# Four graph layers on one core: feed-forward offsets by accumulating DMAs, norm factor on ScalarE, minus the mean on VectorE, a new order table

## The chip, the cores and the metric

The kernel runs on one core of a Trainium2 chip. The metric is the device time of one execution in microseconds. Three executions of the kernel before took 4222.34, 4218.64 and 4213.73 us; the median is 4218.64. The engines are named as in the profile: PE (TensorE, matrix products), DVE (VectorE), ACT (ScalarE), POOL (GpSimd), SP (SyncE, which here only issues DMAs). "PEld" is the loading of weights into the array.

## What is computed

Sixteen graphs `b` of 1024 nodes with 256 features go through four layers that share one 1024 by 1024 adjacency matrix. Each layer has the form `x = x + layer(relu(layernorm(x)))`:

```python
# layers 0, 1 (one head) and 3 (four heads): graph attention
h = x @ W
e = leaky_relu(h @ a1 [:, None] + h @ a2 [None, :])
att = softmax(where(adj, e, -big));  out = relu or elu (att @ h)
# layer 2: eight heads of 32, then a feed-forward part with two norms
q, k, v = split(x @ w_qkv)
t = softmax(where(adj > 0, q @ k.T / sqrt(32), -1e9)) @ v
x = layernorm(x + t) * ln1_g + ln1_b
h = relu(x @ w1 + b1)
x = layernorm(x + h @ w2 + b2) * ln2_g + ln2_b
```

Everything is float32.

## The kernel before

**Stages.** One stage is one layer of one graph, 64 stages in all. The rows of a graph lie as eight tiles of 128 nodes (`NT = 8`), handled in two halves `n` of four tiles (`TH = 4`). The list `order` interleaves the stages: in the middle of the run (2, b), (1, b+1), (3, b), (0, b+2) follow each other, so one period of four stages handles one graph's worth of work, and the way into a stage (norm, transposes, products with the weights) runs under the stage before it.

**Who decides the order.** Nothing is issued directly. Every piece of work is laid down by `op(engine, cost, rank, function, after, ...)`: a planner's record with an engine, an assumed cost in us, what it needs and which buffers it takes. `play` then lists all records in one sequence, and the engines execute their share of it in that order. The sequence comes from `RANKS`, a table of three characters for each record. With another number of records the table cannot be used, so a change that adds or drops records brings a table of its own. The three PSUM double banks (`banks`), the two single ones (`bank`) and eleven large SBUF tiles (`large`) are shared by all stages and are handed out in the planner's order.

**Layer 2.** `dot_item` handles four heads, one tile of keys and one half of queries: eight score products (L1606, `sc`), two exponentials on ACT (L1620), two multiplications with the mask on DVE (L1628), and four products with the values (L1637, `acc`). The softmax sums need the same `pe` tiles again. To halve that work, POOL issues an accumulating DMA for each pair of items (`gather`, L1654: `pe` of the second item is added to `pe` of the first, 1 MB), and one set of products with a column of ones (L1667, `sums`) follows for the pair. There are 16 such gathers for each graph.

**The feed-forward part.** When half `n` of the attention is done, `dot_out` leaves `x + t` in `y`, and `feed_forward` and `finish` run for its four tiles:

- `stats_of`: DVE takes mean and variance (L1051, L1052), POOL makes `(var + eps) ** -0.5` in two instructions (L1055, L1056).
- `affine` on DVE: two instructions of 128 by 256, `(y - mean) * g1` (L1089) and `* rstd + be1` (L1090). `be1` there already holds `ln1_b + b2`, added once at the start; what this adds too much to the product with `w1` is taken off `b1` (`fold_bias`, L1930).
- PE turns the four tiles (L1099), ACT copies them (L1102), PE multiplies with `w1`, ACT applies bias and relu (L1765), PE multiplies with `w2`.
- `finish`: DVE adds the product to `y` with a running sum (L1788), POOL makes minus the mean of it (L1082), ACT the sum of squares about the mean (L1072), POOL the factor (L1075, L1076), DVE the second `affine` (L1089, L1090), and DVE adds the result to `x`, again with a running sum (L1808) for the next layer's norm.

`moments_of` with its POOL instruction L1082 also serves the norms of the layers 1, 2 and 3 on their way in (`way_in`). The running sums that it starts from are written by the last DVE instruction of the layer before (L1417 after layer 0, L1432 after layer 1, L1808 after layer 2).

**At the start**, weights and norm vectors are loaded by SP in four groups; two of the four norm vectors of the feed-forward part are the offsets `be1_sb` and `be2_sb`. **At the end**, the last stage (layer 3 of the last graph) has nothing beside it; DVE makes its weights `p` (L1452) and PE uses them in L1510 and L1486. After the loop six checks are reduced to one flag (L1973 to L1981), and an untaken slow path follows.

Of the kernel before, what the change touches and what calls it, by code (L numbers as in the profile page):

```python
# [26 lines left out]
F32 = mybir.dt.float32  # L27
BF16 = mybir.dt.bfloat16
U8 = mybir.dt.uint8
# [30 lines left out]
    "$;8#QT$Pe#,y#<<#)_#'C#'Z#%^$Qv#$}$%v#*Q#%K#7c#(D#'o#*n#(9#*d$RK#qb$N]$L{#(W#(J#(h#_S#(*#%E#(g#dC$HW#&F#(A#&q#)f"  # L60
    "$<k#)M#%V#'[#(##Xl#+0#X##e.#d}$RJ#+Z#(+#(/#W}#+/#$i#%S#+.#e(#e2#(c#(V#)c$Qy#',$Fn$K^$Cw$AK#()#(f#)v#%D#*J#pc$KY"
    "$=S$E[#)'#WB#)P$P^#),##S#)`#2d#qo#*z#$W#+S$Ey#'c$F%$87#'N#(w#*B#oe#*V$BH#W|$FI#mh#({#)#$(.#_R#*t$FB#WA$Ax##{#(^"
    "#(]$7Z#)S#c:#/i#V?#I*$95#)1#)2$(,$9S$Lu$7`##O$Av$:]#'r#US#-Z#*_#*'#6N#*C#):#+T#*N#+H#*L#*0#dv#*M#+E#)6#)U$(%$Qs"
    "#NY$BA$:E#Oy#&1#)Q#)^#.^$:0#){$#;$:$#)R#FV#'q#)x#)W#18#)p##&#Fi##1#7%#)F#)}#)r#HC#)7##,#4W##:#5?#*&#(L#.[$=U#)o"
    "#hf#+(#-p#)3$@t#*5$PX#aM#*<#)n#J`#pM$:r#)E#*Y##+$LK#*b#*/#'8$8`#D}#/A#*I#*E$O'#bg#ix#W##+?#+=#/;#(Y#)$#AW#7b#GL"
    "#Wy#*i#*a#K'#bf#hF#,;#+-#+G$8##+K#+$$@-#8H#-G#>S#)[#+#$?l#2I$IG#>G#+I#(1#+p$/]#$r#*}$%O#,-$?F#7.#+4#+6$>^#7#$')"
    "#mo#+Q$9c$JB#+b#+M#*4$2&#NJ$&p#*O#$q#mk#pU#/]#6c#+z#{J#z7#*f#%v#n##*v#@4#jM#%/#&P#8u$A5#?[#*u#,*$-p$/+#,>#%$#nN"
    "#68#9Q#+`#+k#+|#n|#,Y$-I#KF#,$$-H#69$7f#,E#,+#,m#,b#,I#,a#,k#+_#,f#,n$9>#,'#,p$-}#,{#,u#*Z#,t#,v#+N#,(#Iq#KI#,g"
    "#)@#Qz#*y#,:#4m#*.#/3#-/#.=#R*#&U#n)$8(#HT#.j#/^#.H#.6#0p#&o$F{#/m$Eu#/$#,4#0t#.h#.Q#Uy#)<#Rl#iY#/)#-a#-&#.p#.3"
    "#(Q#h0#Q.$Jn#-Q$Dc#-B#.>#0X#/d#0M#/g#/`#.k#PQ#.l#.M#GA#/8#/7#%.#p[#,8#-,#-Y#-)#-X#pE#nB#o,#/j#,H$L.$/Z#,P#+j#+<"  # L70
    "#03#-[#05#-7#+]#4>#02$My$=]#,U#@l$8L$4[#,`$)N#,j#3s#+J#-o#,K$8z#,l$Ly#+F#/.$9k#6F#/4#,Z#-s#-$$8;#-A#*q#+U$MK#-C"
    "$LT$@i#*8$=j$9i$;|#,<#-^$LS$E<$ML#,##+m#,}#ZO#+}#^T#-2#*p#,S#27#-F#*6#,O#-1#)l#-0#/+#(I#,c#*P#.8#,)#-x#.c#G`$?%"
    "#Om#.t#,6$>*#,F#P6#-:#0`#*7#&k#,9#7j#/f$;r#0Y#5N#/T#,V#.i#-q#08#.b#0E#*+#0$#*3#0*$<P#C7#2A#-R#'B#-e#.%#,_#-v#,B"
    "#,.#.K#-P#Q=#.{#.P#Q;#.O#.R#P(#.?#.}#Q3#-c#Py#8A#*)#?(#P%#-}#,A$22#--#.L#4v#/O#07#*l#3)#tO$2w#Rz#/V#3i$DF#/U#q)"
    "#0L#[s#/l#/G#^$#0-$G6#.*#0T#pf#/}#K(#/{#gZ#0?#-h#./#.&#q'#=r#q(#0w#*:#zc#(5#2R#3c#,i#,r#34#//#(k#+i$<)#*9#+3#-`"
    "#og#3@#-(#.9#'v#lW#:a#)z#(S#6>#*$#)9#Su#*%#+V#'R#*1#+r$$$#*[$,K#*w#)?#+a$?7#dx#+x$?v#+D#.r$LF#@G#.z#w/#Fx$>K$8t"
    "#(a#,[#*k#Sg#-y#df#,N#/?#-8$Kz#*D$L'#+;#?A#)|#,q#FK#aa#G2#+c$-z#/q#9S#l*#1/#Dd#uE#6:#,0#0;#]G#]F$:f#.-#,3#.4#.:"
    "#.2#.7#.;#.D#TV#mZ#0o#7^#,/#V;#9e#Q%#/K#mY#.S#.m$*,#/:#Un#Q2$Q<#.J#._#.u#.w#Q*#/=$2;$'N$Q;#/a$>m#mg#/H#Z*#/_#Q6"
    "#P_$2v$)w$Q}#Jb#zd#)w#+{#%X#+o#3J#*`#,^#,]#1<#m7#.E#-t#/Q#/-#/<#.0#/E$>r#/2$)1#s+$QV#_0#*##>*#$>#/Y#.|#97#tl#:X"
    "#.,#Vr#3*$Kg$/(#0x$Qm$J*#/w#32#)8#>)#c%#-|#2v$<}$80#/v#3?$7m#{+#0_#z^#oV#ur#+W#0n#4l#ou$PU#0m$';#,5#@6#On#Ro#1Q"  # L80
    "#Ps#DG#&>#.B#1j#1d#0]#1e#p|#.n#z;#1W#.1#/W$3l#ul#A:#1a#@`#0y#1P#/*#0{#0f#.W#0z#fc#-N$C)#G%$K@#0e#2##8j#1k#gz#6r"
    "#17#`c#39#2F#1T#21#/L#/B#/p#2J#0A#2D#1H$2I#2)#2B#2,#/s#2O#1^#0>#/n#1U#/o#2S#0u#1*$,9#1q$<;#2.#/S#2-#.y#1_#/1#bd"
    "#/@#0d#/D#b`#yi#2+#i*#bo#.o#-U#2*#0,##T#0%$=i#T9$9^#3m#i)#ew#/u#gn#E+#.F#8/#1(#/t#0(#0a#0'#2:$FZ#4'#kL#1E#+8#+f"
    "#s5$+*#s1#pN#22#/k#2Y#'*#y]#c}#zN#j*#2t#2f#-{#1:#-w#5t#pL#1I#1h#5}#a@#5k#1D#4G#4K#i%#3-#1S#ZH#19#fn#6G#1i#1F#aK"
    "#7_#fi#5W#]S#2&#gW#3v#m%#fl#-H#a?#7`#2n#15#ZG#7r$RD#;&$Bq#3Z$.7#3W#1o#f*#q-#F&#7s#3X#3B$%S#s.#F%#Q]#rf#yh#j##2r"
    "#$<#4&$,<#vv#QO#3>#3k#5J$)T#5X#QJ$.g#qU#4(#i$#5.#.e#5H$L(#3'#2l#3P#2j#30#2|#3Y#3S#3%$I'#2i#2g$GI#3O#3&#2o#2k#-f"
    "#4i#4V#^z#m.#4?#4L#24#1;#4U#5'#4t#6z#-M#g?#,|#4d#1R#rY#5)#51#+>#.+#gL#-n#(q#4r#Qg$N8#4}#54#4[#28#6j#.'$IO$@j#wr"
    "#5*#5;#4b#A[#4I#3H#1A#7F#0D#2G#66#77#6B#74#3_#5m$=>#5<#5/#6P#5z#5,#1M#pb$,>#w3#P}#7*#?<#0}#;Y#pF#.@#6o#3`#3K$,2"
    "#2W$F8$(3#4D$(}#0P#[r#m,#w.#10#>`$/P#2%#1z#GV#'g#/P$Ka#s$#0B#,C#'f#.N$L&#Li#a8$%@#3a#jG#6C#1)$2t#H|#3$$K`$L7#1G"
    "#LC$O$#3o#2y#2s$Cl#2x#5y#4Z#Ly$2s#5-#1s#@s#45#5P$Dy#4a$;7#5S#4P#2;#qZ$5u#M#$;0#5g$Cm$=5#6'#3}#W8#6@$P<#ei#5f#2>"  # L90
    "#3u#kB#4:#de#46#W`#44#1C#49#1,#e[#2[#_1#JG#6g#8<$*^#4S#y|#)-#I3#)s$*_#4,#3L#*K#I2#4e#7?#yy#6{#8?#1{#3<#/I#57#0&"
    "#5Q#6s#5C#5o#5D#gK#5_#5V#3h#5d#5I#LW#5T#5Y#?E#5+#0c#.#$<x#:|#4X#3y#5B#6*#5>#42#6##6.#41#9;$/Q#kp#6-#9}#43#5w#6H"
    "#5K#9I$1a#^x#6y#6L#:'#.Z#6]#pZ#6h#:Q#6k#:K#6Y#:&#6e#N&#5e#6d#3N#7/#3Q#2c#MI#2]#6;$Op#Yu#70#4h#4g#4w$?[#5c#3A#:q"
    "#sr$>'#S_#5=#G^$/2$1#$Iw#MK#(m#4c#4f#4`#5##4Q#4k#4B$4b$>P#4C#B`#52#56#f8#>}#f:#kA#/z#58#48#5Z#9.#Iw#98#60$?r#1Z"
    "#4)#8N#5v#63#6O$/<$9.#5L#}E#5x$9/#Bj#3]$9-#-j#=`#6$#:{$E'#8Z#3z#MA#6|#9j#5A#59#5G#61#p,$QB#5i#Bm$=^#5F#6b#9_#6T"
# [531 lines left out]
def fast_path(tc, bad, x, adj, l0_w, l0_a, l1_w, l1_a, w_qkv, ln1_g, ln1_b, ln2_g, ln2_b, w1, b1, w2, b2, l3_w, l3_a, out):  # L627
# [13 lines left out]
    with ctx:  # L641
# [1380 lines left out]
```

## Time and profile before

| what | us | where it is from |
|---|---|---|
| median of three executions | 4218.64 | times |
| the profiled execution | 4214.72 | times |
| its span | 4212.7 | page, part 1 |
| DVE busy | 3202.1 | page, part 1 |
| ACT busy | 2272.0 | page, part 1 |
| POOL busy | 1291.4 | page, part 1 |
| mean granted clock of TensorE | 0.996 | clocks and spans by core |

The profiled execution took 2.0 us longer than its span and 3.9 us less than the median. The span runs from the first to the last instruction; sums over the trace are compared with it. Busy time counts an engine as busy from the start to the modelled end of each instruction. Since matmuls follow each other in the array before the earlier ones have ended, a short wait of PE can hide behind the end of the matmul before it; the time from start to start is the safer measure there.

### The profile page before, as it was taken

Reading aid. Unit: us, or ns where it says so; the run is one execution under the profiler, and the core shown is the slowest. Engines: PE = TensorE matmul, PEld = TensorE weight load, DVE = VectorE, ACT = ScalarE, POOL = GpSimd, SP = SyncE. Lnnn points to the kernel's source line nnn. Section 1 sums busy time; section 2 is a strip of 40 time slices with the busy share of each in tenths; the row PEclk is TensorE's granted clock in tenths of the full one; section 3 lists DMA queues with packets and bytes.
Section 4 is the critical chain, followed back from the end, with each engine's and each line's share of the span. In section 5 each row is a group of like instructions: output and inputs, shape, how many; then the busy total and the mean of one; then the engine's idle time right before and its main releaser. Section 6 shows DMA issues by size and latency. Waiting matters only on the chain.

```text
span 4212.7 us, 67513 instructions
## 1 busy us (share of the span) xinstructions
PE 4106.9 (97%) x25993; PEld 2166.0 (51%) x25993; DVE 3202.1 (76%) x5708; ACT 2272.0 (54%) x4107; POOL 1291.4 (31%) x2473
## 2 busy tenths in 40 slices
PE   8999999999999999999999999999999999999997
PEld 7736265553645536455354654546545455564332
DVE  7477877778777787767877778787786777858797
ACT  5563646636465464654646546464563745665452
POOL 3325141422414133142232423223232242424231
PEclk9999999999999999999999999999999999999999
DMA  3061714418053180540805317062260723535261
GB/s 114 16 141 41 158 43 98 93 46 165 21 116 77 45 165 26 115 91 26 165 26 122 85 45 147 26 138 68 62 130 26 154 52 84 107 82 109 70 122 42
DMA packets 96457, 364.35 MB, mean 86 GB/s; under 512 B 10376, under 2 KB 45568, under 8 KB 63360
## 3 DMA queue, kind: packets, MB, share of 16 engines
q0 software_dynamic: 36864, 268.45, 31.7%
q1 hardware_dynamic: 58848, 90.98, 6.3%
q8 instruction: 207, 3.39, 0.3%
q14 instruction: 122, 1.00, 0.1%
q10 hardware_dynamic: 416, 0.52, 0.0%
HBM read 74.32 MB, written 17.17 MB: 22 GB/s over the span
## 4 chain that ended last, share of the span: by engine, by line
PE 76%; DMA 7%; DVE 6%; issue 5%; ACT 3%; POOL 2%; POOLq 0%; ACTq 0%; SPq 0%; DVEq 0%
PE pm L1106 20%; PE av L1388 19%; PE acc L1486 11%; PE sc L1606 7%; DMA pe<-pe 7%; PE acc L1637 6%; PE sums L1510 5%; PE tp L1099 3%; DVE pe L1628 3%; PE sums L1667 3%; ACT pe L1620 1%; POOL rstd L1076 1%; PE tpv L1549 1%; PE tpo L1686 1%; POOL pe L1654 1%
## 5 line engine op out<-in xcount | busy, mean ns | idle before, releaser
L1628 DVE TENSOR_TENSOR pe<-pe,mask 128x1024 f32<-128x1024 f32 x1024 | 1200.6, 1219 | 217.4 <-ACT pe L1620 213.9
L1620 ACT ACTIVATE pe<-sc 128x1024 f32<-128x1024 f32 x1024 | 997.6, 1023 | 331.0 <-PE sc L1606 202.1
L1388 PE MATMUL av<-v,p 128*128 128x257 f32 x4096 | 950.9, 382 | 6.9 <-ACT o L1411 4.3
L1388 PEld LDWEIGHTS av<-v,p 128*128 128x128 f32 x4096 | 760.6, 190 | 194.1 <-issue 56.1
L1452 DVE SCALAR_TENSOR_TENSOR p<-r,e,mask 128x1024 f32<-128x1024 f32 x512 | 622.5, 1273 | 113.4 <-DMA r<-kept 92.0
L1606 PE MATMUL sc<-qT,kT 32*128 32x512 f32 x4096 | 634.0, 641 | 2.7 <-ACT pe L1620 1.2
L1637 PE MATMUL acc<-pe,v 128*32 128x512 f32 x4096 | 543.9, 603 | 3.2 <-DVE pe L1628 1.9
L1654 POOL DMA_DIRECT2D pe<-pe x256 | 225.2, 882 | 933.6 <-PE acc L1637 616.0
L1486 PE MATMUL acc<-p,v 128*32 128x512 f32 x4096 | 467.6, 593 | 0.0
L1082 POOL TENSOR_SCALAR stats<-stats 128x1 f32<-128x1 f32 x512 | 166.4, 333 | 886.0 <-DVE x L1417 564.2
L1606 PEld LDWEIGHTS sc<-qT,kT 32*128 32x128 f32 x4096 | 194.9, 183 | 381.6 <-issue 185.2
L1106 PE MATMUL pm<-l_wx,hT 128*128 128x259 f32 (+1 forms) x1536 | 366.9, 388 | 3.8 <-ACT hT L1102 1.4
L1076 POOL TENSOR_TENSOR rstd<-rstd,minus_half 128x1 f32<-128x1 f32 x512 | 353.4, 690 | 42.7
L1371 DVE SCALAR_TENSOR_TENSOR p<-r,e,mask 128x512 f32<-128x512 f32 x512 | 351.1, 742 | 12.9 <-DMA r<-kept 11.1
L1106 PEld LDWEIGHTS pm<-l_wx,hT 128*128 128x128 f32 x1536 | 287.0, 190 | 74.2 <-ACT hT L1102 19.1
L1667 PE MATMUL sums<-pe,pick 128*32 128x512 f32 x2048 | 272.5, 600 | 39.0 <-DMA pe<-pe 38.3
L1486 PEld LDWEIGHTS acc<-p,v 128*32 128x32 f32 x4096 | 133.0, 110 | 295.2 <-issue 280.4
L1637 PEld LDWEIGHTS acc<-pe,v 128*32 128x32 f32 x4096 | 98.2, 108 | 349.4 <-issue 212.9
L1075 POOL TENSOR_SCALAR rstd<-stats 128x1 f32<-128x1 f32 x512 | 175.0, 342 | 275.6 <-ACT xn L1072 143.3
L1510 PE MATMUL sums<-p,e 128*32 128x512 f32 x2048 | 248.5, 596 | 6.0 <-DVE p L1452 6.0
L1055 POOL TENSOR_SCALAR rstd<-stats 128x1 f32<-128x1 f32 x256 | 94.2, 368 | 478.3 <-DVE stats L1052 472.5
L1106 PE MATMUL pm<-hT,qkv_sb 128*128 128x512 f32 x512 | 231.1, 597 | 2.3 <-ACT hT L1102 2.3
(119 smaller groups left out, 4271.4 us busy)
## 6 DMA issues: line engine op xcount, KB each, us to landing
pe<-pe POOLq DMA_DIRECT2D x256, 1024.0 KB, 8.4
r<-kept SPq DMA_DIRECT2D x64, 512.0 KB
x<-in_x_dram SPq DMA_DIRECT2D x32, 512.0 KB
out_dram<-x SPq DMA_DIRECT2D x64, 256.0 KB
r<-kept SPq DMA_DIRECT2D x62, 256.0 KB
edges<-in_adj_dram SPq DMA_DIRECT2D x8, 512.0 KB
kept<-rows_sb SPq DMA_DIRECT2D x128, 2.0 KB
qkv_sb<-in_L_gnn_w_qkv_dram SPq DMA_DIRECT2D x1, 768.0 KB
```

The source lines that it names most:

```text
L1076: nc.gpsimd.tensor_tensor(rh.t, rh.t, minus_half, ALU.pow)
L1106: nc.tensor.matmul(dst, lhsT=lhsT[:, k, :], rhs=rhs[:, k, :], start=(k == 0), stop=(k == KC - 1))
L1371: nc.vector.scalar_tensor_tensor(ph.t[:, j % each, :], rh.t, s.e[:, j, H + h : H + h + 1], mask[:, j, cols], ALU.max, ALU.mult)
L1388: nc.tensor.matmul(avh.t[:, : s.hs + 1], lhsT=phs[part].t[:, j % each, i * P : (i + 1) * P], rhs=s.v[:, j, h, :], start=(j == 0), stop=(j ...
L1452: nc.vector.scalar_tensor_tensor(ph.t[:, hh, :], s.rh[hp].t[:, hh, :], s.e[:, j, col : col + 1], mask[:, j, :], ALU.max, ALU.mult)
L1486: nc.tensor.matmul(acc[n].t[(2 * hh + part) * W : (2 * hh + part + 1) * W, :], lhsT=s.v[:, jj, h, part * W : (part + 1) * W], rhs=p, start ...
L1510: both(lambda jj, n, hh, h, p: nc.tensor.matmul(sums.t[(2 * n + hh) * W : (2 * n + hh + 1) * W, 0, :], lhsT=s.e[:, jj, 2 * H + h : 2 * H + ...
L1606: nc.tensor.matmul(scs[pair].t[:, hh, :], lhsT=s.kh.t[r0 : r0 + D2, g, j * P : (j + 1) * P], rhs=s.qh.t[r0 : r0 + D2, g, cols], start=True ...
L1620: lambda pair=pair: nc.scalar.activation(part(pair), scs[pair].t, AF.Exp, scale=SCALE2),
L1628: lambda pair=pair: nc.vector.tensor_tensor(part(pair), part(pair), masks(), ALU.mult), [ex], tiles=True,
L1637: nc.tensor.matmul(head(acc, i), lhsT=s.v[:, j, g * QUAD + i, :D2], rhs=ph.t[:, i, :], start=(j == 0), stop=(j == NT - 1))
L1667: nc.tensor.matmul(head(sums, i), lhsT=pick[:, g, :], rhs=th.t[:, i, :], start=first, stop=last)
```

## The change

The reference is unchanged. Six things differ.

- The two offsets of the feed-forward part, `ln1_b + b2` and `ln2_b`, are written once to DRAM as `offsets`, repeated for the four tiles of a half, by eight DMAs of SP. For each half of each graph POOL issues two accumulating DMAs of 512 KB (`offset`): one adds `ln1_b + b2` to the half of `y` after its transposes have been copied, the other adds `ln2_b` to the half of `x` after the tiles have gone through the norm of layer 2. The addition of the product with `w2` waits for the first, the last addition to `x` for the second. `b1` now gets `w1.T @ ln1_b` added.
- First norm of the feed-forward part: DVE keeps `(y - mean) * g1`, which no longer waits for POOL's factor; ACT multiplies with the factor. The second DVE instruction is gone.
- Second norm: DVE keeps `(y - mean) * g2`; the factor is applied in the addition to `x`, which was there before. The second DVE instruction is gone.
- Minus the mean (`mean_of`) is a DVE instruction of one column directly behind the running sum, no longer one of POOL. This holds for the layers 0, 1 and 2.
- Some assumed costs in the planner's records have other values.
- `RANKS` is new: 12154 entries, where there were 12409.

```diff
-        g1_sb, be1_sb = spread(ln1_g, "g1_sb"), spread(ln1_b, "be1_sb")
-        g2_sb, be2_sb = spread(ln2_g, "g2_sb"), spread(ln2_b, "be2_sb")
...
+        g1_sb, g2_sb = spread(ln1_g, "g1_sb"), spread(ln2_g, "g2_sb")
...
+        offsets = dram.tile([2, P, TH, C], F32, name="offsets", bufs=1)
...
-            r_op = op(POOL, 1.15 if shift else 0.85, rank + 0.6, root, [m_op], ends=[mh])
+            r_op = op(POOL, 1.1, rank + 0.6, root, [m_op], ends=[mh])
...
+        def mean_of(mh):
+            nc.vector.tensor_scalar(mh.t[:, 0:1], mh.t[:, 2:3], -1.0 / C, None, ALU.mult)
...
-            m_op = op(
-                POOL, 0.25, rank,
-                lambda: nc.gpsimd.tensor_scalar(mh.t[:, 0:1], mh.t[:, 2:3], -1.0 / C, None, ALU.mult), after,
-            )
-            q_op = op(ACT, 0.45, rank + 0.4, square, [m_op], takes=[rh, *takes], ends=ends)
-            r_op = op(POOL, 1.15 if shift else 0.85, rank + 1.0, root, [q_op], ends=[mh])
+            q_op = op(ACT, 0.49, rank + 0.4, square, after, takes=[rh, *takes], ends=ends)
+            r_op = op(POOL, 1.4 if shift else 1.15, rank + 1.0, root, [q_op], ends=[mh])
...
-        def affine(y, m, r, g, b, op0=ALU.subtract):
-            nc.vector.scalar_tensor_tensor(y, y, m, g, op0, ALU.mult)
-            nc.vector.scalar_tensor_tensor(y, y, r, b, ALU.mult, ALU.add)
...
+        def offset(s, n, which, after, rank):
+            ts = slice(n * TH, (n + 1) * TH)
+            def start():
+                nc.gpsimd.dma_start(out=(s.y, xs[s.b])[which][:, ts, :], in_=offsets[which], accum_op=ALU.add)
+            issued = op(POOL, 0.9, rank, start, after + [offsets_kept], delay=0.6)
+            return op(QUEUE, 2.7, rank, lambda: None, [issued])
...
+                centred = op(
+                    DVE, 0.4, at + 0.6,
+                    lambda yt=yt, mh=mh: nc.vector.scalar_tensor_tensor(
+                        yt(), yt(), mh.t[:, 0:1], g1_sb, ALU.subtract, ALU.mult
+                    ), [m_op] + folded[:1], ends=[mh], takes=[xh, uh] if i == 0 else [], tiles=True,
+                )
                 normed = op(
-                    DVE, 0.96, at + 2.0, lambda yt=yt, mh=mh, rh=rh: affine(yt(), mh.t[:, 0:1], rh.t, g1_sb, be1_sb),
-                    [r_op] + folded, ends=[mh, rh], takes=[xh, uh] if i == 0 else [], tiles=True,
+                    ACT, 0.4, at + 2.0, lambda yt=yt, rh=rh: nc.scalar.activation(yt(), yt(), AF.Copy, scale=rh.t),
+                    [r_op, centred], ends=[rh],
                 )
...
+            shifted = [offset(s, n, 0, [turned], rank + 1.0), offset(s, n, 1, [s.norms[n * TH + i] for i in range(TH)], rank)]
...
-                c = op(DVE, 0.8, rank + 3.7 + 4.0 * u, add, [a], takes=mhs)
+                        mean_of(mh)
+                c = op(DVE, 0.8, rank + 3.7 + 4.0 * u, add, [a, shifted[0]], takes=mhs)
...
+                    def add_scaled(xt=xt, yt=yt, nh=nh, rh=rh):
+                        nc.vector.scalar_tensor_tensor(
+                            xt(), yt(), rh.t, xt(), ALU.mult, ALU.add, accum_out=nh.t[:, 2:3]
+                        )
+                        mean_of(nh)
...
+                        DVE, 0.5, at + 3.0, add_scaled, [centred, r_op, shifted[1]], takes=[nh], ends=[s.yh, rh], tiles=True
...
+        def keep_offsets():
+            for i, row in enumerate((offset_in[:, 0, :], offset_2)):
+                for t in range(TH):
+                    nc.sync.dma_start(out=offsets[i, :, t, :], in_=row)
+        offsets_kept = op(SP, 2.0, 13.0, keep_offsets, [summed] + weights_in[0], ends=[ab_held])
```

In the order that the new table gives, each engine's instructions stand as follows beside the order before. POOL issues the two DMAs for `x` of a graph shortly before its layer 2 begins, the DMA for the first half of `y` between the last but one (or two) gathers of layer 2, and the one for the second half after the last gather. The eight writes of `offsets` stand on SP between the write of the first kept row (L1315 before) and the load of it (L1329 before). PE changes its tile shape 1352 times, before 1332 times; 511 blocks of scores are left, before 504.

## The prediction

> **What bounds the kernel now.** I read the busy times first.
>
> ```profile
> span 4212.7 us, 67513 instructions
> PE 4106.9 (97%) x25993; PEld 2166.0 (51%) x25993; DVE 3202.1 (76%) x5708; ACT 2272.0 (54%) x4107; POOL 1291.4 (31%) x2473
> ```
>
> PE is busy for all but 105.8 us, so no work that the change takes from DVE or POOL can come off the span directly. It pays only where PE waited for it. Hence the list of PE's waits:
>
> ```profile
> PE sums L1667 <- DMA pe<-pe: 38.3, 40, 2.7
> PE tp L1099 <- ACT xn L1160: 9.5, 5, 7.7
> PE count L1980 <- DVE broken L1978: 7.2, 1, 7.2
> PE sums L1510 <- DVE p L1452: 6.0, 2, 5.6
> ```
>
> The largest is for the gathers. This list misses waits that hide behind a matmul's modelled end, so I also costed every PE instruction at its undisturbed pace. The timeline shows the pace: 48 products of 257 columns start within 10.44 us, 217 ns each (0.84 ns a column); four products of a quarter of the array run abreast; a change of tile shape adds 0.09 us, leaving a block of scores 0.21 us, the second pair of scores of an item 0.10 us. All instructions of the trace cost 3996 us that way. PE starts at 7.7 us and the last instructions take 6.5 us; the rest, about 202 us, is waiting. Put to the instruction that started late: 62 us before the 256 groups of gathered sums (L1667), about 40 before scores, 28 before the projections L1106, 21 before L1388, some 25 in the last 130 us. 202 us, 4.8% of the span, is all that any order could win.
>
> Where the waits lie shows in one period (graph 4), cut at its gathers:
>
> ```profile
> core 0: us, PE busy (x) PEld busy (x) DVE busy (x) ACT busy (x) POOL busy (x), PEclk, DMA share, GB/s
> 1216.00:1266.00 50.00, 49.22 (x369) 16.03 (x361) 42.12 (x42) 36.86 (x46) 9.24 (x12) 1.00 0.96 198
> 1266.00:1311.00 45.00, 42.90 (x285) 16.13 (x288) 41.09 (x72) 26.31 (x41) 21.13 (x37) 1.00 0.83 167
> 1311.00:1380.00 69.00, 68.60 (x317) 50.27 (x313) 41.11 (x113) 36.53 (x85) 26.14 (x67) 1.00 0.09 32
> ```
>
> Of the 3.3 us lost, 2.9 fall into layer 2, where the DMA engines are 83 to 96% busy and DVE 84 to 91%. These two, not PE's neighbours in general, are what PE meets.
>
> **The change part by part.** The rows that price it:
>
> ```profile
> L1090 DVE SCALAR_TENSOR_TENSOR y<-y,rstd,be_sb 128x256 f32<-128x256 f32 x256 | 124.2, 485 | 43.1 <-POOL rstd L1076 19.6 <-POOL rstd L1056 0.9 <-POOL rstd L1075 0.9
> L1236 DVE TENSOR_SCALAR both<-e,rstd 128x4 f32<-128x4 f32 (+1 forms) x256 | 50.4, 216 | 66.7 <-ACT e L1231 58.5 <-POOL stats L1082 4.9 <-POOL stats L1078 1.2
> L1160 ACT ACTIVATE xn<-x,stats 128x256 f32<-128x256 f32 x256 | 125.8, 507 | 184.7 <-DVE stats L1052 179.6 <-DMA be_sb<-in_L_gnn_ln_b_dram 0.8
> L1082 POOL TENSOR_SCALAR stats<-stats 128x1 f32<-128x1 f32 x512 | 166.4, 333 | 886.0 <-DVE x L1417 564.2 <-DVE x L1432 135.0 <-DVE y L1788 94.9
> L1654 POOL DMA_DIRECT2D pe<-pe x256 | 225.2, 882 | 933.6 <-PE acc L1637 616.0 <-DVE pe L1628 211.2 <-issue 49.0
> ```
>
> *DVE.* 256 instructions L1090 go. One starts 0.40 us before the next, or 0.57 with the bubble of its dependence on L1089: 102 to 146 us, I take 115. 512 `mean_of` come. No such row exists; the nearest, L1236, takes 0.216 us but lets the next start after 0.08 to 0.13, and a dependent pair adds a bubble: 41 to 118 us, I take 67. Net 48 us less DVE work, between 105 less and 16 more. It lies beside PE everywhere; only the 91% stretch of layer 2 could pass some on. Its 3 us in each graph's stretch against 2.1 us of PE loss give 0 to -10 us; I take -2.
>
> *ACT* gains 128 copies like L1160, 65 us. ACT is 58 to 74% busy in the two stretches above, which covers them. Queued behind a copy that waits for POOL's factor are exponentials, and behind those the masks on DVE; with that cover gone four copies delay each of 32 halves by 2 us at most, on a quarter of them 16 us. I take 0 (0 to +16).
>
> *POOL* loses 512 x 333 ns = 170 us and gains 64 issues at 0.88 us, 56 us. It is 31% busy. The step from running sum to square (L1072) loses an engine change, 0.5 us or so. The chain ends before PE's queue of other work does; 0.
>
> *The offset DMAs in the gathers' queue.* This queue is the dear resource:
>
> ```profile
> q0 software_dynamic: 36864, 268.45, 31.7%
> pe<-pe POOLq DMA_DIRECT2D x256, 1024.0 KB, 8.4
> ```
>
> 31.7% of 4212.7 us over 256 gathers is 5.2 us each, and where gathers queue they are issued 5.2 us apart. 16 of them fill 83 of layer 2's 97 us. By size an offset costs 2.6 us; a price above a gather's 5.2 has no row for it. The two for `x` and the second for `y` fall where no gather is due. The first for `y` stands before the last one or two gathers of each graph. POOL executes in order: while that issue waits for the copied transposes (L1102), the next gather and the factors L1055 and L1075 stand behind it, and behind the gather the sums L1667. In PE work at undisturbed pace, the last three gathers now have 14.8, 14.6 and 12.3 us between the products that free them and their sums (before 11.1, 9.9, 8.9), while the shortest landing is 6.9 us. 2.6 us fit. With the cover gone, 16 x 2.6 = 42 us. I take +2 (0 to +42). The addition L1788 waits for the same DMA, but transposed copy, `w1`, relu and `w2` (0.9 + 3.4 + 0.7 + 3.5 us) lie between.
> The Trainium skill ("DMA: Bandwidth & Descriptors", Anatomy of one DMA) fits such a DMA by 2.0 us plus bytes over 436 GB/s. As an estimate from that page an offset would last 3.2 us and a gather 4.4; the shortest gather here takes 6.9, so the fit is low for accumulation, and by it the +2 stays.
> A rule against the change stands in "SBUF — State Buffer" (the warning on DVE and SWDGE): descriptors of POOL's DMAs cannot be written while certain DVE instructions hold the shared port. L1654's issues here take 850 to 1209 ns with DVE at 84 to 91%. By the rule 64 more issues could each stall an instruction's length; by the row 0.36 us at most.
>
> *SP's eight writes* stand before the load of the row for stage (0, 1). At the 0.4 us that earlier issues of this size take, the load is 3.2 us later, and so the weights that DVE makes of it. PE still has the first stage then: +1 (0 to +4).
>
> *The order table* is the largest part. Three things can be counted in the two orders of instructions.
> Tile shape: 7 more blocks of scores at 0.21 us, 13 other changes at 0.09: +2.7 us.
> Gathers: I binned the 62 us of waits by the PE work between the freeing products and the sums. Under 7 us: 9 groups, 0.9 us of wait each; 7 to 8: 30 at 0.60; 8 to 9: 58 at 0.35; 9 to 10: 62 at 0.16; above: 97 at 0.05. The new order has 3, 14, 57, 59 and 123: 2.7 + 8.4 + 20.0 + 9.4 + 6.2 = 47 us, so -15. Counting also the 5.2 us that each gather holds the queue leaves -5; counting that 27.6 us of the waits stood before the last two gathers, now the roomiest, gives -25.
> PSUM: a block that reuses a bank less than 1.5 us after its last writer lost 0.24 us (82 cases; now 56), scores within 1 us 0.71 (8; now 1): -11; some of these are gathered sums, so -9 (-12 to 0).
> The end: these lines show the last stage.
>
> ```profile
> 4151.12 1.89 PE L1510 MATMUL sums<-p,e 128*32 128x512 f32 x2 [5.58 <-DVE p L1452]
> ...
> 4149.70 31.17 DVE L1452 SCALAR_TENSOR_TENSOR p<-r,e,mask 128x1024 f32<-128x1024 f32 x26
> ```
>
> From the transposed row (4141.1) to the checks PE has 47.5 us of work but DVE needs 32 weights at 1.2 us plus 8.5 us until the row is back, so PE waits 5.6 + 2.3 us and then 0.3 us a dozen times. In the new order 59.5 us of PE work stand behind that transpose, more than DVE's chain takes: -8 (-12 to +3).
>
> **Sum:** 2.7 - 15 - 9 - 8 + 1 - 2 + 0 + 2 = -28 us. On the profiled span 4212.7 that makes 4185 us, 4187 with the 2.0 us around it; that execution lies 3.9 us under the median, which becomes 4190 us. All favourable ends together (-25 - 12 - 12 - 10 + 3) give 4163.
>
> **The rivals.** *Slower, 0.16:* the first `y` offset is the bound. For it speaks that layer 2's queue is already 83 to 96% full and that POOL waits in order; against it that the last gathers now have 12 us or more. It decides once an offset delays the next gather by over 5 us, 12.3 less the 6.9 of a landing. At 5.2 us more than covered on each of 16 graphs it costs 83 us against 30 won: 4270; at half of that, 4230.
> *No change, 0.14:* the distances count PE work alone, and DVE, also nearly full in layer 2, takes over as what ends the waits (L1628 before gathers and `acc`). Then only the end and the tile shapes remain, -8 + 3 + 1: 4215.
> *Much faster, 0.13:* assumed costs nearer to the rows (POOL's factor 1.1, rows 368 + 764 ns; before 0.85) let the table dissolve also the waits that I could not count, before projections and L1388 (49 us) and half of those before scores: 4190 - 40 - 10 = 4140.
> That the change does not do what it says is excluded by the listed order.
>
> **How the numbers follow.** The forecast, 4190, has 0.57; its own range is 4163 to 4209. A measurement tells about 0.2% (8.4 us) from no change. Faster: 0.57 + 0.13 = 0.70, same 0.14, slower 0.16. The range reaches half into the outer cases: 4148 to 4232.
>
> **What would show it.** Right: waits at L1667 under 30 us on the list, the wait for L1452 gone, PE busy unchanged within 10 us, the last gathers of a graph landing before their sums. Wrong: gathers behind the `y` offset landing after 12 us with sums waiting; POOL waiting at that issue for L1102's copies; PE waiting for DVE masks in layer 2; an offset taking as long as a gather.

## The result, and the profile after

| kernel | median us | executions | ratio to before, 95% interval |
|---|---|---|---|
| before | 4215.58 (4211.55 to 4222.34) | 12 | |
| after | 4213.69 (4205.08 to 4220.53) | 12 | 0.9993 [0.9984, 1.0002] |

No change that can be measured; 4190 was forecast. The profiled execution of after took 4213.85 us, 4212.1 of them its span, at a granted clock of 0.994 (the mean share of its full clock that TensorE was given).

The page of after, its first lines and its DMA queue:

```profile
span 4212.1 us, 67534 instructions
...
PE 4093.9 (97%) x25993; PEld 2160.5 (51%) x25993; DVE 3170.0 (75%) x5964; ACT 2322.9 (55%) x4235; POOL 1169.6 (28%) x2025
...
q0 software_dynamic: 46080, 302.01, 36.5%
```

The engines moved as the change says: DVE 32 us less, ACT 51 more, POOL 122 less, 33.6 MB more in the gathers' queue. The span did not move. So work went, and waiting came. The list of PE's waits of after (total us, times, longest):

```profile
PE sums L1658 <- DMA pe<-pe: 27.8, 35, 2.5
PE pm L1097 <- ACT hT L1093: 15.0, 18, 1.4
PE tp L1090 <- ACT xn L1151: 13.3, 9, 7.6
PE av L1379 <- ACT o L1402: 10.7, 9, 5.6
PE tps L1677 <- ACT sums_sb L1668: 7.4, 5, 5.7
PE count L2002 <- DVE broken L2000: 7.2, 1, 7.2
```

(L1658, L1097, L1090, L1379 and L1677 are L1667, L1106, L1099, L1388 and L1686 of before.) The wait for gathers fell from 38.3 to 27.8 and the 6.0 us at the end are gone, both as forecast. New are 10.7 us of `av` for `o` (4.3 before) with a single wait of 5.6, 15.0 of `pm` (5.5 before) and 5.7 of `tps` in one wait. The two lines of before:

```profile
PE pm L1106 <- ACT hT L1102: 5.5, 6, 1.2
PE av L1388 <- ACT o L1411: 4.3, 8, 1.6
```

The list misses waits behind modelled ends, so here is the accounting of the prediction again. It is worked out from the starts in the traces (start to start against the undisturbed pace) and is an estimate, not a view; the column of scores holds about 52 us that are pace, not waiting:

| waiting of PE, us | all | gathered sums | `av` | projections `pm` | `tps` and `tpo` | `acc` | scores | last sums |
|---|---|---|---|---|---|---|---|---|
| before | 254.5 | 62.1 | 20.9 | 27.6 | 9.6 | 8.2 | 93.0 | 9.2 |
| after | 249.0 | 40.7 | 38.3 | 39.1 | 15.6 | 4.1 | 87.6 | 1.6 |
| e1, below | 226.4 | 34.7 | 29.4 | 38.0 | 8.2 | 7.7 | 85.4 | 2.2 |
| e5, below | 235.8 | 51.3 | 24.7 | 39.0 | 10.2 | 3.1 | 83.9 | 1.5 |
| e11, below | 257.8 | 51.8 | 30.9 | 41.5 | 9.2 | 12.0 | 88.2 | 1.5 |

21.4 us before the sums, 7.6 at the end and 5.4 before scores were won; 17.4 before `av`, 11.5 before the projections, 6.0 before `tps` and `tpo` were given back, and 3.0 before the transposed masks, which have no column. All waiting fell by 5.5 us and the span only by 0.6, since the added changes of tile shape take 2.7 us and the part behind PE's last instruction 2.4 more (6.7 us before, 9.1 after).

What makes `av` late is found by following its longest wait, 5.56 us up to 1058.17 us. The chain of waits of after there (start us, length us, what):

```profile
1036.04 14.88 DMA y<-offsets
...
1053.11 0.61 ACT pm L1071 x2
...
1054.78 0.74 DVE p L1362
1055.52 0.41 DVE x L1819 x2
...
1057.75 0.37 ACT o L1402
...
1058.17 5.93 PE av L1379 x13
```

The offset for the first half of `y` takes 14.88 us, and from its landing the chain runs through the addition, the squares, the second norm and `o` into the wait of `av`. POOL's timeline of after (start us, length us, what, and in brackets the idle time before) says why a 512 KB transfer takes so long:

```profile
1030.58 0.86 POOL L1645 DMA_DIRECT2D pe<-pe  x1 [2.70 <-DVE y L1751]
1035.50 0.85 POOL L1645 DMA_DIRECT2D pe<-pe  x1 [4.07 <-PE sc L1597]
1036.04 1.21 POOL L1733 DMA_DIRECT2D y<-offsets  x1
```

It is issued half a microsecond after a 1 MB gather, and three gathers have not landed yet. By the trace they land at 1038.14, 1043.08 and 1048.43 us, some 5 us apart, and the offset 2.5 us behind the last, at 1050.92. And DVE:

```profile
1039.43 5.38 DVE L1362 SCALAR_TENSOR_TENSOR p<-r,e,mask 128x512 f32<-128x512 f32 x8
1051.02 0.42 DVE L1797 SCALAR_TENSOR_TENSOR y<-y,pm 128x256 f32<-128x256 f32 x1 [6.20 <-DMA y<-offsets]
```

Eight masks, then 6.20 us of nothing, then the addition at the moment of landing. The list of DVE's waits says how often that happens:

```profile
DVE y L1797 <- DMA y<-offsets: 17.7, 5, 6.2
```

In 5 of the 16 graphs the first addition starts 0.1 us after the landing of its offset, and DVE had stood for it: 5.5, 1.8, 6.2, 1.6 and 2.6 us in the graphs 1, 2, 3, 12 and 13 (counted from 0). In the other 11 it starts 0.2 to 4.9 us after the landing, held by its product or by DVE's other work. The offset of the first half lands 11.6 us after its issue in the median (5.5 to 17.1); the one for the second half, with no gather ahead, after 5.5 (5.3 to 6.0).
The Trainium skill ("DMA: Bandwidth & Descriptors", Anatomy of one DMA) fits such a DMA by 2.0 us plus bytes over 436 GB/s, as an estimate 3.2 us for 512 KB; the 5.5 us measured alone differ from it, and the fit has no term for what is ahead in the queue, which is the larger part of 11.6.

This wait of PE cost more than its length. The same 16 products `av` behind the wait, in after and then in e1 (below), where that offset is left out:

```profile
1058.17 6.60 PE L1379 MATMUL av<-v,p 128*128 128x257 f32 x16 [5.56 <-ACT o L1402]
```

```profile
1047.74 3.75 PE L1379 MATMUL av<-v,p 128*128 128x257 f32 x16
```

They take 6.60 us in place of 3.75. The granted clock (third column from the right) was 0.50 there in after (1.00 in e1):

```profile
1050.00:1057.20 7.20, 2.61 (x20) 0.74 (x18) 5.33 (x21) 3.42 (x11) 2.93 (x6) 1.00 0.65 134
1057.20:1064.00 6.80, 5.83 (x14) 4.63 (x15) 5.85 (x19) 4.59 (x14) 5.54 (x11) 0.50 0.01 2
```

The clock records of the trace hold 54.2 us at a clock of 0.5 in after, in stretches of 3.4 us or several of that which begin during a wait of PE or shortly behind one; 39.3 us in before, 31.7 in e1. The accounting above counts slow products as waiting.

### The profile page after: what moved, and what is told of

Read it like the earlier page. It is cut to its first block, busy times and chain, and to the rows that moved or that the text cites. A ratio compares the mean times of both kernels' runs of the same rounds, so it can differ in the third digit from the quotient of the medians.

```text
span 4212.1 us, 67534 instructions
## 1 busy us (share of the span) xinstructions
PE 4093.9 (97%) x25993; PEld 2160.5 (51%) x25993; DVE 3170.0 (75%) x5964; ACT 2322.9 (55%) x4235; POOL 1169.6 (28%) x2025
## 4 chain that ended last, share of the span: by engine, by line
PE 74%; DMA 7%; DVE 6%; issue 6%; ACT 4%; POOL 2%; SPq 0%; POOLq 0%; ACTq 0%; DVEq 0%
PE pm L1097 19%; PE av L1379 18%; PE acc L1477 10%; PE sc L1597 8%; PE acc L1628 6%; DMA pe<-pe 5%; PE sums L1501 5%; PE sums L1658 3%; PE tp L1090 3%; DVE pe L1619 2%; DMA y<-offsets 2%; ACT pe L1611 1%; DVE y L1797 1%; ACT pm L1071 1%; PE tpv L1540 1%
## 5 line engine op out<-in xcount | busy, mean ns | idle before, releaser
L1379 PE MATMUL av<-v,p 128*128 128x257 f32 x4096 | 956.7, 384 | 21.7 <-ACT o L1402 10.7
L1379 PEld LDWEIGHTS av<-v,p 128*128 128x128 f32 x4096 | 764.9, 191 | 210.9 <-issue 60.8
L1597 PE MATMUL sc<-qT,kT 32*128 32x512 f32 x4096 | 620.9, 642 | 2.7 <-ACT pe L1611 1.5
L1074 POOL TENSOR_SCALAR rstd<-stats 128x1 f32<-128x1 f32 x512 | 159.0, 311 | 1153.4 <-ACT xn L1071 739.8
L1097 PE MATMUL pm<-l_wx,hT 128*128 128x259 f32 (+1 forms) x1536 | 369.5, 389 | 8.1 <-ACT hT L1093 5.2
L1075 POOL TENSOR_TENSOR rstd<-rstd,minus_half 128x1 f32<-128x1 f32 x512 | 331.6, 648 | 42.7
L1097 PEld LDWEIGHTS pm<-l_wx,hT 128*128 128x128 f32 x1536 | 287.4, 191 | 79.1 <-ACT hT L1093 20.7
L1658 PE MATMUL sums<-pe,pick 128*32 128x512 f32 x2048 | 269.5, 603 | 28.6 <-DMA pe<-pe 27.8
L1051 POOL TENSOR_SCALAR rstd<-stats 128x1 f32<-128x1 f32 x256 | 131.9, 515 | 454.5 <-DVE stats L1048 450.8
L1097 PE MATMUL pm<-hT,qkv_sb 128*128 128x512 f32 x512 | 228.6, 593 | 2.6 <-ACT hT L1093 2.3
L1052 POOL TENSOR_TENSOR rstd<-rstd,minus_half 128x1 f32<-128x1 f32 x256 | 207.8, 812 | 21.3
```

What stands on the lines that cost most here:

```text
L1075: nc.gpsimd.tensor_tensor(rh.t, rh.t, minus_half, ALU.pow)
L1097: nc.tensor.matmul(dst, lhsT=lhsT[:, k, :], rhs=rhs[:, k, :], start=(k == 0), stop=(k == KC - 1))
L1379: nc.tensor.matmul(avh.t[:, : s.hs + 1], lhsT=phs[part].t[:, j % each, i * P : (i + 1) * P], rhs=s.v[:, j, h, :], start=(j == 0), stop=(j ...
L1597: nc.tensor.matmul(scs[pair].t[:, hh, :], lhsT=s.kh.t[r0 : r0 + D2, g, j * P : (j + 1) * P], rhs=s.qh.t[r0 : r0 + D2, g, cols], start=True ...
L1658: nc.tensor.matmul(head(sums, i), lhsT=pick[:, g, :], rhs=th.t[:, i, :], start=first, stop=last)
```

## The experiments

All are edits of after unless said otherwise; ratios are to the kernel before, run on the same chip (after: 0.9993). An edit's change against after is the difference of the ratios times 4216 us.

**e1 and e2: leave DMAs out.**

```diff
             def start():
+                if which == 0 and n == 0:
+                    return
                 nc.gpsimd.dma_start(...)
```

e2 has the `return` without the condition.

> The accumulating DMA of the first half of y is left out in every graph (ln1_b + b2 is not added there); the order of everything else is the changed kernel's. Theory A (that DMA lands behind one or two gathers, 10 to 17 us after its issue, DVE stands at L1797 until it lands, and the work behind DVE's wait makes PE late): about 25 us less than the changed kernel, 4190 us, DVE's idle time before the addition down from 85 to about 50 us, PE's waits before L1379 down from 38 to about 20 us. Theory B (the ACT copies and the table itself cause the new waits): within 6 us of the changed kernel, 4208 to 4218. Theory C (the DMA's 2.6 us in the queue delay the gathers behind it): the gain shows at the gathered sums, not at L1379.

> All 64 accumulating DMAs are left out (the offsets are not added); order as in the changed kernel. Theory A: the same as without the first y DMA alone, within 4 us, about 4188, since the other 48 land alone in 5.4 us where nothing waits long. If the traffic itself counts (theory C): at least 8 us less than without the first y DMA alone.

e1: 4188.41 us, 0.9937 [0.9920, 0.9953]. e2: 4190.12, 0.9943 [0.9927, 0.9960]. So the 16 transfers for the first half of `y` cost 0.9993 - 0.9937, about 24 us, and the other 48 nothing that can be measured. Theory A's time was met; DVE's idle time (69.8 us, below) and `av` in the accounting (29.4 us) fell less than it said. DVE's rows for the addition, after and then e1 (busy us, mean ns, idle before and its releasers):

```profile
L1797 DVE SCALAR_TENSOR_TENSOR y<-y,pm 128x256 f32<-128x256 f32 x128 | 52.9, 413 | 85.4 <-PE pm L1097 67.4 <-DMA y<-offsets 17.7 <-ACT pm L1071 0.2
```

```profile
L1799 DVE SCALAR_TENSOR_TENSOR y<-y,pm 128x256 f32<-128x256 f32 x128 | 52.9, 414 | 69.8 <-PE pm L1097 69.5
```

The 17.7 us of standing for the DMA are gone and 2.1 us come back as waiting for the product (67.4 to 69.5), so DVE stands 15.6 us less. By the accounting `av` wins 8.9 us, `tps` and `tpo` 7.4, the gathered sums 6.0.

**e3: the offsets added by DVE**, with one 128x1024 instruction at the place where the DMA was issued. This is the whole computation.

```diff
+                if which == 0 and n == 0:
+                    nc.vector.tensor_tensor(s.y[:, ts, :], s.y[:, ts, :], off_sb.unsqueeze(1).to_broadcast([P, TH, C]), ALU.add)
+                    return
```

> In the place of the DMA of the first half of y, DVE adds ln1_b + b2 with one instruction of 128 x 1024 (some 1.2 us, 16 times); all is computed. Theory A: it keeps most of the gain, 8 to 20 us less than the changed kernel, 4195 to 4206, less than both kernels; what is lost against leaving the DMA out is at most DVE's 16 x 1.2 = 19 us. Theory B: 4213 or up to 10 us more.

4194.18 us, 0.9950 [0.9933, 0.9967]: 0.5% less than before and 0.4% less than after. The 16 instructions take 1.22 us each, 19.5 us in all, and cost 6 us against e1.

**e4: minus the mean back on POOL**, in after's order (`mean_of` on `nc.gpsimd`).

> Minus the mean goes back to POOL (512 instructions of some 333 ns), at the same places of the order; all is computed. Theory A: this part of the change is worth little, 0 to 12 us more than the changed kernel. If the 512 small DVE instructions (79 us of DVE) are what gave the gain back: 10 to 25 us less than the changed kernel.

4249.02 us, 1.0084 [1.0067, 1.0100], 38 us slower than after: missed. The releasers of e4's second norm:

```profile
L1819 DVE SCALAR_TENSOR_TENSOR x<-y,rstd,x 128x256 f32<-128x256 f32 x128 | 61.5, 483 | 40.2 <-POOL rstd L1075 38.2
```

DVE now stands 38.2 us for POOL's factor there (11.7 in after), and PE's wait of `tp` for `xn` grew from 13.3 to 24.9 us.

**e5: the first half's DMA into a scratch area**, so that the queue carries it but nobody waits.

```diff
+                first = which == 0 and n == 0
+                to = spare_rows if first else (s.y, xs[s.b])[which][:, ts, :]
-                nc.gpsimd.dma_start(out=(s.y, xs[s.b])[which][:, ts, :], ...)
+                nc.gpsimd.dma_start(out=to, ...)
```

> The changed kernel, with the first half's accumulating DMA of the rows y kept in its place in the order and with its 512 KB, but aimed at a scratch area in DRAM instead of y; the 16 offsets of that half are left out of y, so that part of the computation is missing. Theory A (the VectorE queue standing at the addition until the offset lands): nothing waits for the scratch, so the time is that of the kernel without these DMAs, 4188 +/- 6 us, VectorE's idle time before the addition is about 70 us and not 85. Theory C (the 512 KB themselves hold the gathers' queue up and the gathers behind it come late): 4213 +/- 6 us, with the sums' wait for the gathered rows at 28 us as in the changed kernel.

4202.17 us, 0.9971 [0.9959, 0.9982]: between the two theories, 9 us under after. `av` fell to 24.7 us as if the DMA were gone, but the sums' wait for gathers rose to 51.3. The transfer into the scratch area, in DRAM, lands after 14.1 us in the median. Its issue also stands closer behind a gather (0.5 to 0.6 us in 15 graphs, in after in 7), and in the one graph with no gather ahead it landed after 5.5 us, as in after. So the two queues are not the same: the run shows that both halves of the price exist, not how large each is.

**e6: the factor of the first norm on DVE.**

```diff
-... nc.scalar.activation(yt(), yt(), AF.Copy, scale=rh.t),
+... nc.vector.tensor_scalar(yt(), yt(), rh.t, None, ALU.mult),
```

> The changed kernel, with the factor of the first norm multiplied in on VectorE at the place where ScalarE does it (128 instructions of 128x256). ScalarE is relieved of 128 x 0.50 = 64 us, VectorE gets about 128 x 0.3 to 0.4 = 38 to 53 us more. Theory A (VectorE's standing still is what costs): VectorE has less to spare, so 0 to 25 us slower than the changed kernel, 4213 to 4240 us. Theory D (ScalarE's 65 us of added work makes o late, and av waits for it): 10 to 25 us faster, 4188 to 4204 us, with av's wait for o down from 10.7 us to under 5.

4224.37 us, 1.0020 [1.0011, 1.0029], 11 us slower, inside theory A's range; `av`'s wait for `o` stayed at 10.3 us. So ACT's added copies are not what made `o` late.

**e7 and e10: the offset in other places.** e7 lets DVE multiply and add in one instruction instead of ACT's copy; e10 is e3 with `nc.gpsimd`.

```diff
+  (lambda ...: nc.scalar.activation(yt(), yt(), AF.Copy, scale=rh.t)) if n else
+  (lambda ...: nc.vector.scalar_tensor_tensor(yt(), yt(), rh.t, off_sb, ALU.mult, ALU.add)),
```

> The whole computation. In the first half of each graph VectorE multiplies the factor in and adds the two offsets in one instruction, in place of ScalarE's copy and of the DMA; the first bias is kept in two forms so that the second bias may be in the row already. The second half is that of the changed kernel. Theory A: no wait for an offset in the first half, 64 x 0.41 = 26 us more on VectorE, 64 x 0.50 = 32 us less on ScalarE: 4184 to 4196 us. Theory C says the same. If VectorE's busy time is the limit, 4205 us or more.

> Whole computation. In the first half of each graph GpSimd adds the two offsets to the four rows with one 128x1024 instruction at the DMA's place; no DMA for this half. On VectorE the same instruction took 1.22 us and the kernel 4194 us. Nothing here shows what GpSimd takes for it. Theory A: no queue behind gathers; if it takes under 5 us the offset comes sooner than by the DMA (10 to 17 us) and the time is 4188 to 4200 us; if GpSimd takes longer, the gathers' issues behind it are late and it is 4205 us or more.

e7: 4204.14, 0.9972 [0.9962, 0.9982]. e10: 4205.26, 0.9974 [0.9964, 0.9985]. Both missed upward by 5 us or more. In e7 PE waits 8.9 us for `pe` and 5.1 us for `y` on DVE: the instruction stands ahead of masks and waits for POOL's factor. In e10 POOL takes 4.14 us where DVE took 1.22, so the offset is there before the DMA would have brought it, but `av` still waits 37.5 us in the accounting (of an execution 8.6 us above e10's median). What made e7 and e10 slower than e3 is not shown further.

**e8: minus the mean on DVE in the kernel before**, nothing else (L1082 on `nc.vector`).

> The kernel before, with minus the mean on VectorE instead of GpSimd and nothing else changed. GpSimd loses 512 x 0.33 = 170 us, VectorE gets 512 x 0.154 = 79 us. In the changed kernel's order the opposite step cost 35 us. Theory E (that work on GpSimd is late wherever it stands): 15 to 40 us faster than before, 4175 to 4200 us. Theory F (the 35 us were the price of an order table written for VectorE; each order is right for its own engine): from 0 to 30 us slower than before, 4215 to 4245 us.

4213.22 us, 0.9997 [0.9988, 1.0006]: no change, far from theory E and, within the interval, at the lower edge of theory F (no loss). The step whose reversal costs 38 us in after's order gains nothing in before's.

**e9 and e12: let DVE do other work first.** A pass behind the planner moves the addition's record, and what depends on it, past the next 4 or 8 DVE records that do not need it.

```diff
+            while sum(o.eng == DVE for o in passed) < c.late:
+                x = row[i]
+                if earlier[x] & moved or any(h.ring in rings for h in x.takes):
+                    moved.add(x)
+                    held.append(x)
...
+                else:
+                    passed.append(x)
+                i += 1
+            row[at:i] = passed + held
```

> The changed kernel, whole computation, with all 64 DMAs. Behind the planner a pass moves the record of the first addition in each graph's first half (and whatever depends on it) past the next 4 VectorE records that do not need it. Theory A (what costs about 19 of 25 us is other VectorE work standing behind the waiting addition; about 6 us are the gathers held up by the DMA and stay): 4 records of about 0.4 to 3 us pass ahead, so part of the 19 us comes back, 4198 to 4208 us. Theory G (the addition's own chain, squares, second norm, way into layer 3, is what is late): 4213 us or more.

> As the one before, past 8 VectorE records. Theory A: most of the 19 us comes back, 4192 to 4202 us, and VectorE's idle time before the additions that is put down to the DMA is under 6 us (17.7 in the changed kernel). Theory G: 4215 us or more, slower than with 4 records.

4253.97 us, 1.0094 [1.0080, 1.0108], and 4298.06, 1.0192 [1.0178, 1.0206]. The pass moved the first pair of additions only. The second pair waits for the same DMA and stood where it had been, so DVE stood nearly as in after (17.4 and 12.2 us put to the DMA), while the last addition of the half started 3.3 and 6.5 us later than in after, counted from the landing. So these two price lateness with little or no relief. e12 moves both pairs.

> The changed kernel, whole computation, with all 64 DMAs. In each graph's first half both pairs of additions, and what depends on them, move past the next 4 VectorE records that do not need them. VectorE's idle time before the additions that is put to the DMA should fall from 17.7 us to under 10. Theory A (other VectorE work behind the waiting addition): 4196 to 4210 us. Theory G (the addition's own chain): what the chain loses is the 2 to 3 us by which the additions come later than they would, less what they stood anyway: 4220 to 4255 us, with more waiting of tps and tp for sums_sb and xn.

> As the one before, past 8 records. Idle time put to the DMA under 5 us. Theory A: 4190 to 4205 us. Theory G: about twice the loss of the run with 4 records, 4235 to 4300 us.

4311.23 us, 1.0222 [1.0205, 1.0239], and 4354.40, 1.0329 [1.0312, 1.0347]. The first of them, by DVE's row and PE's waits:

```profile
L1820 DVE SCALAR_TENSOR_TENSOR y<-y,pm 128x256 f32<-128x256 f32 x128 | 52.7, 412 | 65.7 <-PE pm L1120 65.5 <-ACT pm L1094 0.2
```

```profile
PE tp L1113 <- ACT xn L1174: 79.5, 47, 7.7
PE sums L1681 <- DMA pe<-pe: 32.4, 41, 2.9
```

DVE no longer stands for the DMA at all, and the kernel is 97 us slower than after. The first additions now start 7.5 us (10.6 with 8 records) after the landing on average, in after 1.6, and the transposes `tp` wait 79.5 us for `xn` of the next stage (13.3 in after). Both runs lie above theory G's own ranges too, by some 55 us: the additions came later than the 2 to 3 us that it reckoned with. The four runs side by side:

| run | last addition of the half later than in after, us a graph | slower than after, us a graph | per us |
|---|---|---|---|
| e9, 4 records | 3.3 | 2.7 | 0.81 |
| e9, 8 records | 6.5 | 5.2 | 0.81 |
| e12, 4 records | 6.5 | 6.0 | 0.93 |
| e12, 8 records | 9.9 | 8.9 | 0.89 |

The second column counts from the landing of the offset, the third is (ratio - 0.9993) x 4216 / 16. If DVE's standing in itself cost time, e12, which is rid of it, would lose less for each microsecond than e9; it loses no less. So theory A has nothing for it here, and theory G fits: the chain from the first half's additions onward has little slack, and each microsecond by which it is late costs 0.8 to 0.9. The moved piece holds ACT's and POOL's records of that chain too, so the slope is that of the whole chain. It also holds the slower clock: e12 has 160.1 and 184.4 us at a clock of 0.5 (after 54.2; the means are 0.982, 0.979 and 0.994), an estimated 53 and 65 us of PE's time, half of the difference, out of 97 and 142 us lost.

**e11: the offset ahead of the gather.** In each graph the gather that stands directly ahead of the first offset is issued directly behind it.

```diff
+            for c in [o for o in row if o.kind == "offset"]:
+                at = row.index(c)
+                i = max(j for j in range(at) if row[j].kind == "gather")
...
+                row[i : at + 1] = stay + [c] + moved
```

> The changed kernel, whole computation, with all 64 DMAs. In each graph the gather that stands directly ahead of the first half's offset on GpSimd is issued directly behind it instead; nothing else is moved. Theory A and theory G agree that it is the late landing that costs (about 19 of 25 us): with one 1024 KB gather less ahead, the offset lands about 5 us sooner (5 to 12 us after its issue instead of 9.6 to 17.1), which gives back most of the 19 us, and the 16 moved gathers land some 3 us later each, of which up to 16 us may show as more waiting of the sums: 4196 to 4212 us, with av's wait for o under 6 us. If the traffic in the queue is what costs, and not the landing, the time stays at 4213 us or above.

4219.69 us, 1.0007 [0.9998, 1.0016]: missed, and by its own words a sign for the traffic; the table behind this run takes landing and traffic apart. POOL and DVE of e11 in the same graph as above:

```profile
1027.75 0.86 POOL L1750 DMA_DIRECT2D y<-offsets  x1 [1.73 <-DVE pe L1635]
1030.09 0.86 POOL L1661 DMA_DIRECT2D pe<-pe  x1 [1.48 <-DVE pe L1635]
```

```profile
1034.02 5.38 DVE L1378 SCALAR_TENSOR_TENSOR p<-r,e,mask 128x512 f32<-128x512 f32 x8
1040.30 0.42 DVE L1815 SCALAR_TENSOR_TENSOR y<-y,pm 128x256 f32<-128x256 f32 x1 [0.90 <-DMA y<-offsets]
```

The mechanism did what was expected: the offset lands 6.9 us after its issue in the median instead of 11.6, DVE stands 0.90 us instead of 6.20 here, `av` waits for `o` 5.3 us instead of 10.7. The gain went elsewhere: the sums are back at 51.8 us and `acc` at 12.0. One of those waits alone is

```profile
3864.77 1.93 PE L1675 MATMUL sums<-pe,pick 128*32 128x512 f32 x8 [9.29 <-DMA pe<-pe]
```

in the one graph where the gather had to be moved far, 16.4 us behind its predecessor; without it the run would be about level with after (an estimate). Either the addition or a gather is second in that queue, and both are on the path.

**Where the time lies, graph by graph.** PE runs the same products in the same order in after and in each of the runs below (at least 25985 of 25993 records agree place by place). So the start of one product in after, less its start in another run, is that run's lead. The table has what the lead gained from 15 us before to 22 us after the landing of the offset in after, for the five graphs in which DVE stood, and what it gained everywhere else (profiled executions, graphs counted from 0):

| us | graph 1 | graph 2 | graph 3 | graph 12 | graph 13 | everywhere else | difference of the spans |
|---|---|---|---|---|---|---|---|
| DVE stood in after | 5.5 | 1.8 | 6.2 | 1.6 | 2.6 | | |
| e1, no transfer | 7.2 | 2.2 | 7.1 | 0.5 | 4.5 | 2.4 | 23.9 |
| e2, no offsets at all | 7.0 | 2.5 | 7.1 | 0.6 | 4.0 | 7.4 | 28.6 |
| e3, added by DVE | 7.0 | 0.3 | 6.5 | 0.6 | 3.4 | 1.2 | 19.0 |
| e5, into scratch | 7.2 | -2.2 | 7.1 | 0.5 | 3.3 | -2.8 | 13.1 |
| e11, ahead of the gather | 6.9 | 0.4 | 6.7 | 0.6 | 4.3 | -27.6 | -8.7 |

21.5 of e1's 23.9 us are won in these five graphs, 18.8 of them in three. Every way of sparing the addition its wait wins nearly the same in the graphs 1, 3 and 13, also e5, which still moves the 512 KB, and e11, which still adds them by DMA; those two lose elsewhere, e11 10.7 us at the long wait above. In after, PE has 17.1 us at a clock of 0.5 within 7 us of the landing in the graphs 1, 3 and 13; none of the five other runs has any there.

## Why the prediction was wrong, step by step

**The step that failed** is the sentence on the addition: "The addition L1788 waits for the same DMA, but transposed copy, `w1`, relu and `w2` (0.9 + 3.4 + 0.7 + 3.5 us) lie between". The 8.5 us themselves were not far off: in the five graphs in which DVE stood, it had come to the addition 8.7 to 11.6 us after the issue (landing less standing). But they were held against no landing behind gathers. The same paragraph had the numbers: 5.2 us for each gather in the queue, and the offset "before the last one or two gathers", so behind the others. In these graphs it landed 10.4 to 17.1 us after the issue, behind up to three gathers. The term "+2 (0 to +42)" measured 24 us (e1), inside its range but for another reason: the range came from gathers delayed behind the offset. 21.5 us of it lie at the five waits of the addition: 17.7 us of standing, which the chain passes on to `o`, `av` and `tps`, and up to 8.5 us (an estimate, half of 17.1 us) of PE at half clock behind three of them, less what PE made good. The 6.0 us of the gathered sums lie partly in the same places and cannot be added to this.

**The rival "slower"** watched the right queue from the wrong side: the gather behind the offset. It was held to decide from 5 us of delay on; e1 shows 6.0 us of sums in all. It and the term set 12.3 us against the shortest landing of a gather, 6.9; the median in the same lines is 8.4.

**Gathers, -15:** 62.1 to 40.7, -21, and 34.7 without the offset, -27. That lies inside its range of 5 to 25 (e1 just outside); no run tests the binning by itself.

**The end, -8:** 9.2 to 1.6, -7.6. **PSUM, -9:** the waits before scores fell by 5.4; not separated further.

**ACT 0, DVE -2 and POOL 0:** no run takes these apart from the new table. In after's order, putting the factor back on DVE costs 11 us (e6), minus the mean back on POOL 38 (e4). For minus the mean this is no gain over before (e8: nothing). One reading is that the new table is fitted to its engines and before's order had room for POOL; that is argued, not shown. The 48 other offsets at nothing are right within what can be measured (e2).

**The sum** without its failed term was right within 6 us: -30 forecast, and 0.9943 (e2), 24 us under before. That agreement is in part luck: single terms were off in both directions, and the 10.4 us that the projections lost even in e1 (27.6 to 38.0) stood in no term.

**The signs.** "An offset taking as long as a gather" stood in the list of what would prove the forecast wrong, and it is what the trace shows (11.6 us to the landing, a gather 8.7). Two of the signs of being right appeared too: 27.8 us of waits at the sums, and no wait for the last stage's weights. So those two say nothing about the step that failed. PE's busy time fell by 13.0 us, outside the 10 that were allowed.

## What to carry to other kernels

Here a transfer landed after what was ahead of it in its queue: before a DMA takes over an engine's work, work out its landing from the place of its issue, and hold that against the first instruction that needs it. An engine that stands waiting need not be the cost in itself; ask whether what it waits for starts a chain with slack, and test it by letting the engine do something else first. The full queue here passed a delay from one user to the other (e5, e11), so a short piece of work on an engine with time left (e3, 1.22 us) can be cheaper than a free-looking transfer. Where two runs share an order, subtract the starts of the same instructions: a loss that looks like 1.5 us a graph can be 7 us in three of them.

## What the runs showed of the hardware

- An accumulating DMA of 512 KB from DRAM to SBUF lands 5.5 us after its issue in the median in the second half of `y`, with no gather ahead, and 11.6 us in the first half, 15 times of 16 behind gathers. Where three gathers had not landed at its issue, it took 14.7 to 17.1 us (four graphs).
- The granted clock of TensorE fell to 0.5 for 3.4 us or several of that during or shortly behind waits of PE: 16 products of 257 columns took 6.60 us in place of 3.75. After has 54.2 us of this, e12 with 8 records 184.4.
- An addition over 128x1024 float32 took 1.22 us on VectorE and 4.14 us on GpSimd; one of 128x1 took 0.154 and 0.300 us.
